# A twelve-slot loop under a hand-written lane schedule: three slots of rest after the reciprocal root, statistics and normalising in pairs of tiles, one scaling step on GpSimd, and another background pace

## The chip, the cores and the metric

The kernel runs on one core of one Trainium2 chip. The metric is the device time of one execution in microseconds (us); the time before is 6226.83 us, the median of 5 runs (6213.99 to 6240.11).

## The reference, cut to what matters

Eight images of 128 channels and 36 by 36 positions pass through a convolutional attention layer (layer 0), and then, as 1296 tokens of 128 channels, through an additive attention and a gated mixture of experts (layer 1).

```
x = x + conv_attention(group_norm(x))            # 3x3 convolutions, softmax attention, tanh
t = to_tokens(x)
t = t + additive_attention(layer_norm(t))        # softmax over j of sum_d w_d tanh(q_id + k_jd)
t = t + experts(layer_norm(t))                   # 64 experts, each takes its 8 likeliest tokens
x = from_tokens(t)
```

The experts' gating takes a softmax over the 1296 tokens for each expert, keeps the 8 largest probabilities and uses them as weights.

## The kernel before, in words

**The main loop.** The additive attention is written as sums of fractions: a denominator and a numerator, both matrix products of exponentials of queries and keys. It is cut into 8 images (`b`), 3 chunks of 432 queries (`c`) and 11 key tiles (`j`). Such a unit has 12 *slots*, the short eleventh tile (16 keys, placed sixth in the order) has 3, so an image has 3 x (10 x 12 + 3) = 369 slots and the kernel 2952. Slots are numbered here from 0 to 368 within an image; slots 60 to 62, 183 to 185 and 306 to 308 are the short ones. In each slot `p` the program emits:

1. `take_turns(p)`: steps of the background work that need no matmul (VectorE, ScalarE, GpSimd),
2. `numerators(p)`: PE products into two PSUM tiles `n`, from a ring `ps_n` of 4 that the background's PSUM tiles (`aux`) share,
3. `denominators(p + 3)`: PE products into a tile `d`, then on ScalarE a logarithm `lq` (line 872) and, in every second slot, exp(-lq) for both (line 875),
4. `terms(p)`: VectorE multiplies `n` by `lq`. In the slots 0, 1, 3, 4, 6, 7, 9, 10 of a unit the two results `rp` (line 903, ring of 3) are added by GpSimd (lines 908, 910); in the slots 2, 5, 8, 11 (`DVE_PAIRS`) VectorE adds them itself (lines 892 to 899),
5. `matmul_turn(p)`: steps of the background work that start with matmuls.

Each engine runs its instructions in the order in which they were emitted, so a step that waits holds up all that stands behind it on that engine.

**The background work.** While image `b` goes through the main loop, lanes of Python generators emit the rest of the work a step at a time: the gating of image `b - 1` (lane `gates`), and for image `b + 1` in turn `normal`, `conv_keys`, `layer0`, `tokens` and `keys` (lane `background`). A generator says with each `yield` what it wants next: `step(r)` is a step without matmuls after `r` slots of rest, `matmuls(r)` a step that begins with matmuls after `r` slots, `TAKE` is `step(1)`. Every background matmul adds its columns plus 20 to a counter; `matmul_turn` lets one group through when the balance is not negative, and gives the balance `PACE` columns back in each slot:

```
            before = behind[0]
            for lane in lanes:
                while lane.due(p, True) and behind[0] == before:
                    if lane is not first_of_all and balance[0] < 0 or lane is gates and urgent:
                        break
                    lane.run(p)
            balance[0] = min(balance[0] - (behind[0] - before) + PACE, PACE)
```

`layer0(b + 1)` emits nothing until the gating of `b - 1` is through. Image 0 is prepared ahead of the loop; the last image's gating, and the experts, come behind it.

**The parts that the change touches.** `tokens` turns an image into tokens: 11 transposes (`tpl`) in groups of 4 tiles, copies into `tok` (line 558), then for each of the 11 tiles a `bn_stats` and a `bn_aggr` on VectorE (lines 573, 574), with a `step()` behind every third tile; then `ve` (variance plus epsilon, line 216), two slots of rest, the reciprocal root `ln_rs` on GpSimd (line 221), transposes `tpn` and the normalising `xh` on VectorE (line 593), four tiles at a time, then the transposes `tpc` and copies `xT` (line 610). `gate_logits` does the like with the attention's result: `tp3`, and the normalising at line 739, four tiles at a time, once for each of the three chunks. `gate_tokens` has the softmax over tokens: the maximum `nm` (line 766), an exp on ScalarE with its sum (line 769), a reciprocal `ginv` (line 772), the scaling of the 64 x 1296 probabilities `probs` on ScalarE (line 774), the 8 largest (`Max8`, line 777) and their replacement (line 780) on VectorE, and a difference on GpSimd (line 782). The tanh of `layer0` (line 464, between two loads of ScalarE's function tables) is not touched; neither is `normal`, whose `xwin` (lines 353 to 357) are GpSimd additions.

Of the kernel before, what the change touches and what calls it, by code (L numbers as in the profile page):

```python
# [10 lines left out]
AF = mybir.ActivationFunctionType  # L11
ALU = mybir.AluOpType
AX = mybir.AxisListType

NB, C, H, W = 8, 128, 36, 36
# [7 lines left out]
T = 108  # L23
NT = N // T
TPC = CH // T
KT = [(j, min(128, N - j)) for j in range(0, N, 128)]
NKT = len(KT)
# [28 lines left out]
LAG = 3  # L56
SHIFT = 6.5
DVE_PAIRS = (2, 5, 8, 11)
PACE = 350

REM_SLOTS = [([q + m for m in range(NF // 2)], rows) for q, rows in SLOTS[:3]]

# [2 lines left out]
def kernel(  # L65
# [28 lines left out]
    nc = tc.nc  # L94
# [21 lines left out]
    ident = const.tile([128, 128], F32, tag="ident", name="ident")  # L116
# [4 lines left out]
    with ExitStack() as loop, ExitStack() as score:  # L121
# [22 lines left out]
        def big_tile(name):  # L144
            return big.tile([128, NT * 128], F32, tag="big", name=name)
# [4 lines left out]
        def aux(name):  # L150
            return ps_n.tile([128, 512], F32, tag="n", name=name)
# [76 lines left out]
        TAKE = (False, 1)  # L228

        def step(rest=1):  # L230
            return (False, rest)

        def matmuls(rest=0):
            return (True, rest)
# [7 lines left out]
        def turned_to(out, in_, identity):  # L242
            behind[0] += 148
            nc.tensor.transpose(out, in_, identity)
# [294 lines left out]
        def tokens(b):  # L539


            r = xs.pop(b)
            tok = big_tile("tok")[:, : NKT * C].rearrange("p (t c) -> p t c", c=C)
            st = small.tile([128, NKT, 6], F32, tag="ln_st", name="ln_st")
            mv = small.tile([128, NKT, 2], F32, tag="ln_mv", name="ln_mv")
            nc.gpsimd.memset(mv, 1.0)
            yield matmuls(2)
            for g in range(0, NKT, 4):
                tp = aux("tpl")
                some = list(range(g, min(g + 4, NKT)))  # L550
                for t in some:
                    o, n = KT[t]
                    turned_to(
                        tp[:n, (t - g) * C : (t - g + 1) * C], r[:, o : o + n], ident
                    )
                yield TAKE
                full = sum(KT[t][1] == 128 for t in some)
                nc.vector.tensor_copy(
                    tok[:, g : g + full, :],
                    tp[:, : full * C].rearrange("p (t c) -> p t c", c=C),  # L560
                )
                for t in some[full:]:
                    n = KT[t][1]
                    nc.vector.tensor_copy(tok[:n, t, :], tp[:n, (t - g) * C : (t - g + 1) * C])
                yield matmuls()
            full = N // 128
            nc.sync.dma_start(
                tokd[b][: full * 128].rearrange("(t p) c -> p t c", p=128), tok[:, :full, :]
            )
            o, n = KT[-1]  # L570
            nc.sync.dma_start(tokd[b][o : o + n], tok[:n, NKT - 1, :])
            for t, (o, n) in enumerate(KT):
                nc.vector.bn_stats(st[:n, t, :], tok[:n, t, :])
                nc.vector.bn_aggr(mv[:n, t, :], st[:n, t, :])
                if t % 3 == 2:
                    yield step()
            ve = plus_eps(mv[:, :, 1], 1e-5, [128, NKT])
            yield step(2)
            rs = small.tile([128, NKT], F32, tag="ln_rs", name="ln_rs")
            rsqrt(rs, ve)  # L580
            xh = big_tile("xh")[:, : NKT * (C + 1)].rearrange("p (t c) -> p t c", c=C + 1)
            nc.gpsimd.memset(xh[:, :, C : C + 1], 1.0)
            yield matmuls()
            for g in range(0, NKT, 4):
                tp = aux("tpn")
                some = list(range(g, min(g + 4, NKT)))
                for t in some:
                    o, n = KT[t]
                    turned_to(tp[:n, (t - g) * C : (t - g + 1) * C], r[:, o : o + n], ident)
                yield TAKE  # L590
                for t in some:
                    n = KT[t][1]
                    nc.vector.tensor_scalar(  # L593
                        xh[:n, t, :C], tp[:n, (t - g) * C : (t - g + 1) * C],
                        mv[:n, t, 0:1], rs[:n, t : t + 1], ALU.subtract, ALU.mult,
                    )
                yield matmuls()
            xT = big_tile("xT")[:, :N]
            yield matmuls(2)
            for g in range(0, NKT, 4):  # L600
                tp = aux("tpc")
                some = list(range(g, min(g + 4, NKT)))
                for t in some:
                    o, n = KT[t]
                    turned_to(
                        tp[:, (t - g) * 128 : (t - g) * 128 + n], xh[:n, t, :C], ident[:n, :n]
                    )
                yield TAKE
                lo, hi = KT[g][0], KT[some[-1]][0] + KT[some[-1]][1]
                nc.vector.tensor_copy(xT[:, lo:hi], tp[:, : hi - lo])  # L610
                yield matmuls()
            xr = two.tile([128, C + 1], F32, tag="xr", name="xr")
            for i in range(TPC):
                nc.sync.dma_start(xr[32 * i : 32 * i + REM], xh[:REM, NKT - 1, :])
            prepared[b] = (xh, xT, xr)
# [39 lines left out]
        def attend(b, c, es):  # L655
# [38 lines left out]
            if b == NB - 1:  # L694
                yield from gate_logits(b, [c])
# [7 lines left out]
        def gate_logits(b, chunks):  # L703


            t2, mv = attended[b]
            if b not in logits:
                logits[b] = (
                    big_tile("probs")[:E, :N],
                    small.tile([E, NCH], F32, tag="mx", name="mx"),  # L710
                )
            pr, mx = logits[b]
            tiles = range(chunks[0] * TPC, (chunks[-1] + 1) * TPC)
            yield step()
            ve = plus_eps(mv[:, tiles[0] : tiles[-1] + 1, 1], 1e-5, [T, len(tiles)])
            yield step(2)
            rs = small.tile([T, len(tiles)], F32, tag="t2_rs", name="t2_rs")
            rsqrt(rs, ve)
            yield matmuls()

            def turned(c, name):
                tp = aux("tp2")
                for j in range(TPC):
                    turned_to(tp[:, j * T : (j + 1) * T], t2[:T, c * TPC + j, :], ident[:T, :T])
                return tp, chunk_tile(name)

            for c in chunks:
                tp, tt = turned(c, "t2T")
                yield TAKE
                nc.vector.tensor_copy(tt, tp[:, :CH])  # L730
                nc.sync.dma_start(t2d[b][:, c * CH : (c + 1) * CH], tt)
                yield matmuls(1)
                tp = aux("tp3")
                for j in range(TPC):
                    turned_to(tp[:T, j * C : (j + 1) * C], tt[:, j * T : (j + 1) * T], ident)
                yield TAKE
                for j in range(TPC):
                    t = c * TPC + j
                    nc.vector.tensor_scalar(
                        t2[:T, t, :], tp[:T, j * C : (j + 1) * C],  # L740
                        mv[:, t, 0:1], rs[:, t - tiles[0] : t - tiles[0] + 1],
                        ALU.subtract, ALU.mult,
                    )
                yield matmuls(1)
            for c in chunks:
                tp, xc = turned(c, "xc")
                yield TAKE
                nc.vector.tensor_copy(xc, tp[:, :CH])
                yield matmuls(2)
                pg = aux("pg")  # L750
                bmm(pg[:E, :CH], gw_s, xc, start=True, stop=True)
                yield TAKE
                nc.vector.tensor_scalar(
                    pr[:, c * CH : (c + 1) * CH], pg[:E, :CH], gb_s, None, ALU.add, ALU.max,
                    accum_out=mx[:, c : c + 1],
                )
                yield matmuls()

        def gate_tokens(b):


            t2, _ = attended.pop(b)
            pr, mx = logits.pop(b)
# [7 lines left out]
            inv = small.tile([E, 1], F32, tag="ginv", name="ginv")  # L771
            nc.vector.reciprocal(inv, tot)
            yield step()
            nc.scalar.activation(pr, pr, AF.Copy, scale=inv)
            yield step(2)
            top = small.tile([E, 8], F32, tag="top", name="top")
            nc.vector.max(out=top, in_=pr)
            yield step()
# [8 lines left out]
            for g in range(2):  # L787
                tp = aux("tpg")
                for j in range(half):
                    t = g * half + j  # L790
# [172 lines left out]
        def matmul_turn(p):  # L963
# [3 lines left out]
# [7 lines that stand above are left out]
# [17 lines left out]
        for p, (u, k) in enumerate(slots):  # L991
            b, c, j = units[u]
# [216 lines left out]
```

## Time and profile before

| what | value |
|---|---|
| time, median of 5 runs | 6226.83 us |
| the profiled execution's own time | 6213.99 us |
| its span | 6212.3 us |
| mean granted TensorE clock | 0.974 |
| PE busy | 5972.8 us (96%) |
| ScalarE (ACT) busy | 5348.4 us (86%) |
| VectorE (DVE) busy | 4831.3 us (78%) |
| GpSimd (POOL) busy | 4698.0 us (76%) |

The profiled execution was the fastest of the five. Engine times are of instructions that overlap in a pipeline, so a busy PE need not be working at its peak. The granted clock is the share of TensorE's full clock that the chip let it have; it is either 1 or one half at any moment of this profile. A main-loop unit with no background work at all is found in the last image, where nothing is left to prepare.

### The profile page before, as it was taken

Reading aid. Unit: us, or ns where it says so; the run is one execution under the profiler, and the core shown is the slowest. Engines: PE = TensorE matmul, PEld = TensorE weight load, DVE = VectorE, ACT = ScalarE, POOL = GpSimd, SP = SyncE. Lnnn points to the kernel's source line nnn. Section 1 sums busy time; section 2 is a strip of 40 time slices with the busy share of each in tenths; the row PEclk is TensorE's granted clock in tenths of the full one; section 3 lists DMA queues with packets and bytes.
Section 4 is the critical chain, followed back from the end, with each engine's and each line's share of the span. In section 5 each row is a group of like instructions: output and inputs, shape, how many; then the busy total and the mean of one; then the engine's idle time right before and its main releaser. Section 6 shows DMA issues by size and latency. Waiting matters only on the chain.

```text
span 6212.3 us, 108419 instructions
## 1 busy us (share of the span) xinstructions
PE 5972.8 (96%) x41064; PEld 2930.5 (47%) x41064; DVE 4831.3 (78%) x9595; ACT 5348.4 (86%) x5426; POOL 4698.0 (76%) x2868
## 2 busy tenths in 40 slices
PE   7899999999999999999999999999999999999996
PEld 5454455544554445544445444554445444544443
DVE  3687778877788777887788787887778878788872
ACT  1799998998989989899898998899888998999980
POOL 3678877787788877888687786778777887778870
PEclk9999999999999999999999999999999999999997
DMA  1210021100110001100111001110011000100018
GB/s 43 70 36 22 23 66 38 34 25 28 58 52 23 26 30 65 37 27 23 50 45 42 22 21 62 41 36 22 24 65 48 24 26 27 59 31 29 25 58 272
DMA packets 158892, 272.37 MB, mean 44 GB/s; under 512 B 53857, under 2 KB 83425, under 8 KB 158369
## 3 DMA queue, kind: packets, MB, share of 16 engines
q1 hardware_dynamic: 158368, 265.44, 13.0%
q8 instruction: 323, 5.29, 0.4%
q14 instruction: 201, 1.64, 0.1%
HBM read 200.94 MB, written 64.19 MB: 43 GB/s over the span
## 4 chain that ended last, share of the span: by engine, by line
PE 75%; DVE 9%; ACT 6%; issue 6%; POOL 2%; DMA 1%; SPq 0%; DVEq 0%; POOLq 0%; ACTq 0%
PE n L850 36%; PE d L850 11%; PE pa L240 7%; PE pc L240 5%; ACT lq L872 4%; DVE n L897 3%; PE s L240 3%; PE pk L240 3%; PE pq L240 2%; DVE rp L903 2%; DVE accd L899 1%; PE n L857 1%; PE d L857 1%; POOL accp L910 1%; DMA w<-in_weight_dram 1%
## 5 line engine op out<-in xcount | busy, mean ns | idle before, releaser
L910 POOL TENSOR_TENSOR accp<-accp,rp 128x864 f32<-128x864 f32 x1464 | 2966.2, 2026 | 1006.7 <-DVE rp L903 942.2
L850 PE MATMUL n<-qf,kf 32*128 32x432 f32 (+1 forms) x11520 | 3279.0, 575 | 63.0 <-DVE xh L593 14.5
L872 ACT ACTIVATE lq<-d 128x864 f32<-128x864 f32 x2952 | 2552.9, 882 | 504.5 <-PE d L850 461.6
L850 PE MATMUL d<-qf,kf 32*128 32x432 f32 (+1 forms) x11520 | 2874.3, 565 | 39.4 <-ACT lq L872 34.8
L903 DVE TENSOR_TENSOR rp<-n,lq 128x432 f32<-128x432 f32 x3984 | 2198.5, 600 | 562.1 <-PE d L850 392.9
L875 ACT ACTIVATE lq<-lq 128x1728 f32<-128x1728 f32 x1488 | 2430.0, 1633 | 47.1
L850 PEld LDWEIGHTS n<-qf,kf 32*128 32x128 f32 (+1 forms) x11520 | 1186.0, 185 | 1605.0 <-DVE rp L903 451.0
L850 PEld LDWEIGHTS d<-qf,kf 32*128 32x128 f32 (+1 forms) x11520 | 1031.5, 187 | 406.1 <-issue 230.9
L897 DVE TENSOR_TENSOR n<-n,lq 128x432 f32<-128x432 f32 x1440 | 811.9, 609 | 263.9 <-PE n L850 228.9
L899 DVE TENSOR_TENSOR accd<-n,accd 128x432 f32<-128x432 f32 x1440 | 868.0, 603 | 24.7
L908 POOL TENSOR_TENSOR accp<-rp 128x864 f32<-128x864 f32 x264 | 534.4, 2024 | 145.5 <-DVE rp L903 143.7
L917 POOL TENSOR_TENSOR accp<-accp 128x432 f32<-128x432 f32 x264 | 291.7, 1105 | 17.6
L648 POOL TENSOR_SCALAR qf<-qf,cs_s 128x432 f32<-128x432 f32 x192 | 261.3, 1367 | 43.2 <-ACT qf L647 43.2
L240 PEld LDWEIGHTS pa<-xh,e 128*108 128x108 f32 x1920 | 223.6, 175 | 131.2 <-DVE rp L903 76.6
L920 POOL TENSOR_TENSOR accd<-accp,accd 128x432 f32<-128x432 f32 x240 | 266.0, 1108 | 21.9 <-DVE accd L899 3.8
L240 PE MATMUL pa<-xh,e 128*108 128x129 f32 x1920 | 262.8, 284 | 10.3 <-DVE accd L899 6.1
L892 DVE TENSOR_TENSOR accd<-n,lq 128x432 f32<-128x432 f32 x240 | 144.8, 603 | 113.3 <-PE n L850 83.5
L240 PE MATMUL s<-q,k 128*116 128x432 f32 x480 | 230.3, 568 | 2.2 <-DVE q L272 1.4
L426 ACT ACTIVATE e<-s 116x432 f32<-116x432 f32 x240 | 125.0, 521 | 119.0 <-PE s L240 118.7
L240 PEld LDWEIGHTS pk<-xT,a_k 128*128 128x128 f32 x1408 | 171.7, 193 | 106.7 <-issue 27.5
L417 POOL TENSOR_TENSOR tot<-tot,e 116x432 f32<-116x432 f32 x192 | 212.3, 1106 | 6.7 <-ACT e L426 4.5
L240 PE MATMUL pa<-e,vw 116*128 116x432 f32 x480 | 204.6, 549 | 2.8 <-DVE accd L899 2.8
(202 smaller groups left out, 3963.8 us busy)
## 6 DMA issues: line engine op xcount, KB each, us to landing
kf<-kd SPq DMA_DIRECT2D x240, 512.0 KB
kd<-ks SPq DMA_DIRECT2D x160, 256.0 KB
w<-in_weight_dram SPq DMA_DIRECT2D x32, 1024.0 KB
wk_t<-wk_t_d SPq DMA_DIRECT2D x7, 768.0 KB
wv_t<-wv_t_d SPq DMA_DIRECT2D x7, 768.0 KB
wq_t<-wq_t_d SPq DMA_DIRECT2D x7, 768.0 KB
x<-in_x_dram SPq DMA_DIRECT2D x8, 648.0 KB
t<-tokd SPq DMA_DIRECT2D x96, 54.0 KB
```

What stands on the lines that cost most here:

```text
L240: mm(out, lhsT, rhs, **kw)
L648: nc.gpsimd.tensor_scalar(qf[:, 1, :], qf[:, 0, :], cs_s[:, q : q + 1], None, ALU.mult)
L850: mm(outs[h][:, :CH], kf[rows[h], q, :], qf_of[b, c, q][rows[h], part, :], start=True, stop=True)
L872: nc.scalar.activation(lq[:, o : o + 2, :], d[:, :, :CH], AF.Ln)
L875: nc.scalar.activation(some, some, AF.Exp, scale=-1.0)
L897: mult(ns[h], ns[h], lq[:, o + h, :])
L899: nc.vector.tensor_add(live["d"], ns[h], live["d"])
L903: mult(rp[:, h, :], ns[h], lq[:, o + h, :])
L908: nc.gpsimd.tensor_add(live["p"], live["r"], rp)
L910: nc.gpsimd.tensor_add(live["p"], live["p"], rp)
L917: nc.gpsimd.tensor_add(s[:, 0, :], s[:, 0, :], s[:, 1, :])
L920: nc.gpsimd.tensor_add(d, s[:, 0, :], d)
```

## The change

In `tokens`, the statistics pass on after every second tile; three slots lie between the reciprocal root and the first normalising transposes (none before), and transposing and normalising go two tiles at a time. In `gate_logits`, the normalising goes two tiles at a time. In `gate_tokens`, the scaling of the probabilities is a GpSimd instruction for all images but the last, and three slots lie behind it in place of two. `PACE` goes from 350 to 365 columns a slot.

```diff
-PACE = 350
+PACE = 365
...
                 nc.vector.bn_stats(st[:n, t, :], tok[:n, t, :])
                 nc.vector.bn_aggr(mv[:n, t, :], st[:n, t, :])
-                if t % 3 == 2:
+                if t % 2 == 1:
                     yield step()
...
             nc.gpsimd.memset(xh[:, :, C : C + 1], 1.0)
-            yield matmuls()
-            for g in range(0, NKT, 4):
+            yield matmuls(3)
+            for g in range(0, NKT, 2):
                 tp = aux("tpn")
-                some = list(range(g, min(g + 4, NKT)))
+                some = list(range(g, min(g + 2, NKT)))
...
-                tp = aux("tp3")
-                for j in range(TPC):
-                    turned_to(tp[:T, j * C : (j + 1) * C], tt[:, j * T : (j + 1) * T], ident)
-                yield TAKE
-                for j in range(TPC):
-                    t = c * TPC + j
-                    nc.vector.tensor_scalar(
-                        t2[:T, t, :], tp[:T, j * C : (j + 1) * C],
-                        mv[:, t, 0:1], rs[:, t - tiles[0] : t - tiles[0] + 1],
-                        ALU.subtract, ALU.mult,
-                    )
-                yield matmuls(1)
+                for j0 in range(0, TPC, 2):
+                    tp = aux("tp3")
+                    for j in (j0, j0 + 1):
+                        turned_to(tp[:T, j * C : (j + 1) * C], tt[:, j * T : (j + 1) * T], ident)
+                    yield TAKE
+                    for j in (j0, j0 + 1):
+                        t = c * TPC + j
+                        nc.vector.tensor_scalar(
+                            t2[:T, t, :], tp[:T, j * C : (j + 1) * C],
+                            mv[:, t, 0:1], rs[:, t - tiles[0] : t - tiles[0] + 1],
+                            ALU.subtract, ALU.mult,
+                        )
+                    yield matmuls()
...
-            nc.scalar.activation(pr, pr, AF.Copy, scale=inv)
-            yield step(2)
+            if b == NB - 1:
+                nc.scalar.activation(pr, pr, AF.Copy, scale=inv)
+            else:
+                nc.gpsimd.tensor_scalar(pr, pr, inv, None, ALU.mult)
+            yield step(3)
             top = small.tile([E, 8], F32, tag="top", name="top")
             nc.vector.max(out=top, in_=pr)
```

## The prediction

> **What bounds the kernel now.** I read the page first, then cut the loop into its units (the starts of line 872, one a slot, give the borders) and asked for busy times and granted clock in each. The windows view gives, in order: a unit without background (last image), and in image 3 the units of slots 294 to 305 (tanh), 309 to 320 (statistics, normalising), 48 to 59 (gating's softmax) and the short unit behind it.
>
> ```profile
> core 0: us, PE busy (x) PEld busy (x) DVE busy (x) ACT busy (x) POOL busy (x), PEclk, DMA share, GB/s
> 5740.08:5760.04 19.96, 19.25 (x98) 7.68 (x98) 16.73 (x32) 19.77 (x20) 16.61 (x10) 1.00 0.08 27
> 2984.92:3015.02 30.10, 26.51 (x352) 12.04 (x348) 21.53 (x40) 25.67 (x24) 18.00 (x13) 0.89 0.09 33
> 3020.91:3051.41 30.50, 26.36 (x115) 12.13 (x110) 24.81 (x66) 21.18 (x21) 19.45 (x13) 0.78 0.16 48
> 2499.36:2524.29 24.93, 24.87 (x363) 12.86 (x360) 22.48 (x44) 23.52 (x23) 23.18 (x20) 1.00 0.09 29
> 2524.29:2534.34 10.05, 9.53 (x152) 5.56 (x150) 4.61 (x10) 4.13 (x4) 5.34 (x4) 0.66 0.05 12
> ```
>
> A bare unit is ScalarE's: 19.77 of 19.96 us. With background a unit lasts 21 to 25 us, bound by whichever engine has most in it; PE's 96% hides that. Two units stick out at 30 us, and the clock falls there: 0.78 over 30.50 us is 2 x 0.22 x 30.5 = 13.4 us at half clock. The unit of the change is the third row. Its chain is in the timeline (image 2's copy of it, VectorE then GpSimd) and the waits:
>
> ```profile
> 2288.37 1.13 DVE L897 TENSOR_TENSOR n<-n,lq 128x432 f32<-128x432 f32 x2 [0.59 <-PE n L850]
> 2289.40 1.24 DVE L899 TENSOR_TENSOR accd<-n,accd 128x432 f32<-128x432 f32 x2
> 2293.15 1.37 DVE L593 TENSOR_SCALAR xh<-tpn,ln_mv,ln_rs 128x128 f32<-128x128 f32 x4 [2.50 <-POOL ln_rs L221]
> ```
>
> ```profile
> 2286.89 4.12 POOL L910 TENSOR_TENSOR accp<-accp,rp 128x864 f32<-128x864 f32 x2 [2.94 <-DVE rp L903]
> 2290.97 2.15 POOL L221 TENSOR_TENSOR ln_rs<-ve,neg_half 128x11 f32<-128x11 f32 x1
> ```
>
> ```profile
> DVE xh L593 <- POOL ln_rs L221: 20.0, 8, 2.7
> ```
>
> The root stands behind two additions on GpSimd, VectorE stands 2.5 us before `xh` with the main loop's products behind it, and PE then stands 2.4 us (the largest gaps before it are 1.16 and 0.71 us, behind the statistics). All 8 images wait so.
>
> **Part 1, tokens.** Work is unchanged: 11 x (0.266 + 0.182) = 4.9 us of statistics and 11 x 0.40 = 4.4 us of `xh`. Before, VectorE has 24.81 us to do in the 30.50: 5.7 us over, of which 2.5 is the wait and 3.2 the half clock and the gaps.
> - Rest: the root has three slots (about 6 us against 2.15 plus two additions of 2.03). The wait of 2.5 goes. Next late is VectorE itself: 9.3 main + 4 us for the six slots of `xh`, which is about what it does now.
> - Pairs of `xh`: 0.8 us a slot in place of 1.6. With the wait gone I let the second half-clock stretch go, half of 3.2 less gaps: -1.6. Six `aux` tiles instead of three tighten the ring `ps_n`; bounds -0.3 to +1.5, taken 0, since VectorE is the limit there.
> - Statistics: the built order shows six tiles in a row become four (not two: one turn is run by `matmul_turn`, the next by the following `take_turns`), then twos. 2.4 us of burst become 1.6, 1.2 become 0.8: -1.2 of gaps.
> - Against it: the statistics now stand in slots 300 to 304, with no background up to slot 309. VectorE has 13.6 us for six slots (9.0 main, 4.6 statistics) where PE alone would take 10: a half-clock stretch is likely to stay and now reaches the short unit 306 to 308. What a stretch costs there: the short unit 60 to 62 lasts 7.0 us in image 2 (clock 1), 10.05 in image 3. Bounds 0 to +3, taken +1.3.
> Sum: -2.5 - 1.6 - 1.2 + 1.3 = -4.0 us an image, bounds -7 to -1. The tanh unit (third of a stretch of the same kind) only moves, nine slots ahead.
>
> One rule on the clock differs from these rows. The Trainium skill (TensorE: Matmul & The Clock Gate, "HAM oscillation — how this bites in real kernels") asks for PE gaps over about 3.4 us before the clock falls. Here it falls after gaps of 1.16 and 0.71 us, so gaps alone don't decide. By the page no clock would be won, and part 1 would be -2.5 - 1.2 = -3.7.
>
> **Part 2, gating's normalising.** Slots 24 to 35 last 24.9 us in image 2 (clock 1) and 26.6 in image 3 (6.8 us at half clock). Four `L739` of 0.402 in a row, among three `bn_stats` of 0.6, become twos. The stretch was full in three images of six; -0.7, bounds -1.7 to +0.5. The transposes use the same slots (28 to 37), so gating is not later: `tpg` at slot 65, before 66.
>
> **Part 3, the scaling.** ScalarE loses 1.36 us in a unit where it is busy 23.52 of 24.93: -1.0. GpSimd gains a one-input pass over 1296 columns, which the trace lacks. Nearest rows:
>
> ```profile
> L648 POOL TENSOR_SCALAR qf<-qf,cs_s 128x432 f32<-128x432 f32 x192 | 261.3, 1367 | 43.2 <-ACT qf L647 43.2
> L782 POOL TENSOR_TENSOR gt<-probs,gt 64x1296 f32<-64x1296 f32 x7 | 20.6, 2937 | 0.0
> ```
>
> Three times the first is 4.1 us, the second 2.9. I take 3.6 (1.367 x 2.937/1.105, the width's ratio taken from lines 782 and 917). GpSimd is behind there, in GpSimd's, ScalarE's and VectorE's timelines:
>
> ```profile
> 2512.67 4.13 POOL L910 TENSOR_TENSOR accp<-accp,rp 128x864 f32<-128x864 f32 x2
> ```
>
> ```profile
> 2517.43 1.36 ACT L774 ACTIVATE probs<-probs,ginv 64x1296 f32<-64x1296 f32 x1
> ```
>
> ```profile
> 2519.56 1.49 DVE L777 MAX8 top<-probs 64x8 f32<-64x1296 f32 x1
> ```
>
> The scaling is emitted behind the additions that end at 2516.8; the last `xwin` group comes a slot later than before, so I place their end at 2517.5 and the scaling's at 2521.1. `Max8` stays in slot 59 and could start at 2519.4: VectorE stands 1.7 us (0.3 to 3), with slot 59's products behind it, and PE's `n` behind those. The half clock in the short unit, full in two of six images and half in two, becomes the rule: +1.2. Sum +1.9, bounds -1 to +5. In the last image no `xwin` is in the way: 0.
>
> A page prices it otherwise. The Trainium skill (GPSIMD Engine Reference, "4.1 Engine selection") holds one-input passes to be roughly line rate there, which would be an estimate of 1.5 us from the `Max8` row; then nothing waits, the part is -1.0, and the whole would be near 6189.
>
> **Part 4, pace.** Columns don't change (117752 an image), their places do. In the built order `keys` ends at slot 357, not 363. Units with the same load in the trace give the exchange: slots 270 to 281 fall from 4520 to 3164 columns (25.3 to 22.3 us, -3.0), slots 345 on give another -1.5; units at 75, 87, 123, 147, 186 and 246 take 390 to 820 more, worth +0.2 to +1.5 each, +4.8 together, and the smaller moves -0.9. Sum -0.6, bounds -3 to +3.
>
> **Sum.** -4.0 - 0.7 + 1.9 - 0.6 = -3.4 us in each of images 1 to 6, -20 us in all. Image 0 has no gating (part 1 gain and pace loss cancel), image 7 has no tokens: 0 each. The profiled time 6214.0 becomes 6194; it lies 12.8 below the median of 6226.8, so on that scale 6206.
>
> **Rivals.**
> - *GpSimd becomes the wait (slower).* Place: slot 59. It decides once the scaling ends 3 us or more after VectorE arrives. Then part 3 is +5, the half clock stays behind the statistics (part 1 -1.5) and pace gives +0.5: 6 x 4 = +24, 6251; milder forms end near 6242. For it: GpSimd 23.18 of 24.93 us busy before the addition. Against: the rest is three slots. Chance 0.25.
> - *All half clock goes.* Statistics in twos keep PE fed, `Max8` doesn't wait: part 1 -7, part 2 -1, part 3 -0.5, pace 0: -8 x 6 = -48, 6179 to 6190. For it: short gaps triggered these stretches. Against: 13.6 us of VectorE in six slots. Chance 0.22.
> - *The change doesn't thin the bursts enough.* Four tiles in a row and an idle background keep the stretch: part 1 -2, the rest as forecast: -1.4 x 6 = -8, 6218. Chance 0.19.
>
> **How the numbers follow.** The forecast of 6206 has 0.34. About 0.2% (12.5 us) is what a measurement of this kernel can tell from no change: below 6214 is faster, over 6239 slower. Faster 0.34 + 0.22 = 0.56; same 0.19; slower 0.25. The range reaches from the second rival's low end to the milder forms of the first: 6178 to 6246.
>
> **What would show it.** Right: no wait of `xh` for `ln_rs`; the unit of slots 309 to 320 at 24 to 25 us with a clock of 1; the mean clock up from 0.974 to about 0.98; the scaling at 3.5 to 4.1 us with a wait of `Max8` for it near 1.7. Wrong: a wait of `Max8` over 3 us, the clock at half in slots 300 to 308 in every image for 6.8 us, or units at 75 to 250 longer by more than 5 us in sum.

## The result and the profile after

| | before | after |
|---|---|---|
| time, median (runs) | 6226.83 us (57) | 6238.84 us (32) |
| profiled execution, span | 6212.3 us | 6250.2 us |
| mean granted clock | 0.974 | 0.972 |

The ratio is 1.0018, 95% interval 1.0011 to 1.0024: some 11 us slower, where 6206 had been forecast. The profiled execution of before lies 12.8 us below its median, that of after 13.2 us above; 26 of the 38 us between the two traces are scatter.

The windows view of after, in the order of the rows shown of before (bare unit; image 3: 294 to 305, 309 to 320, 48 to 59, the short unit 60 to 62), with the unit of slots 24 to 35 as a last row:

```profile
core 0: us, PE busy (x) PEld busy (x) DVE busy (x) ACT busy (x) POOL busy (x), PEclk, DMA share, GB/s
5801.54:5821.50 19.96, 19.25 (x98) 7.68 (x98) 16.73 (x32) 19.77 (x20) 16.34 (x10) 1.00 0.08 27
3004.73:3029.59 24.86, 23.27 (x351) 11.63 (x347) 24.26 (x60) 21.32 (x21) 16.08 (x11) 0.93 0.21 68
3036.18:3058.86 22.68, 22.42 (x122) 10.88 (x119) 21.42 (x45) 20.67 (x21) 18.45 (x12) 1.00 0.11 32
2509.79:2536.25 26.46, 26.29 (x364) 13.87 (x360) 22.51 (x44) 22.44 (x22) 26.18 (x23) 1.00 0.09 31
2536.25:2543.21 6.96, 6.43 (x152) 3.68 (x150) 4.64 (x10) 4.13 (x4) 5.31 (x4) 1.00 0.02 5
2460.44:2488.17 27.73, 25.16 (x120) 11.70 (x120) 26.23 (x54) 20.95 (x20) 20.65 (x13) 0.94 0.13 43
```

The unit of the change, 309 to 320, went from 30.50 to 22.68 us, with the clock at 1. Unit 24 (slots 24 to 35) did not get shorter; before, it was in this image:

```profile
2450.80:2477.44 26.64, 24.96 (x124) 11.80 (x121) 24.62 (x54) 20.80 (x20) 19.66 (x12) 0.87 0.25 92
```

VectorE's waits, and the scaling in the groups and in GpSimd's and VectorE's timelines:

```profile
DVE xh L593 <- POOL ln_rs L221: 2.3, 1, 2.3
DVE top L781 <- POOL probs L778: 1.2, 6, 0.2
```

```profile
L778 POOL TENSOR_SCALAR probs<-probs,ginv 64x1296 f32<-64x1296 f32 x7 | 24.9, 3554 | 0.0
```

```profile
2527.92 3.55 POOL L778 TENSOR_SCALAR probs<-probs,ginv 64x1296 f32<-64x1296 f32 x1
```

```profile
2531.51 1.50 DVE L781 MAX8 top<-probs 64x8 f32<-64x1296 f32 x1 [0.19 <-POOL probs L778]
```

The 20 us wait of `xh` is down to one of 2.3 (image 0), and `Max8` waits 0.2 us a time. To see where the time went I summed the unit lengths by stretch of an image (borders are again the starts of the logarithm's line), the mean of images 1 to 6, in brackets the time at half clock:

| kernel | 0-23 | 24-62, gating | 63-281 | 282-320, tokens | 321-368 | image |
|---|---|---|---|---|---|---|
| before | 45.5 | 81.2 (8.0) | 428.9 (0.6) | 88.4 (18.8) | 97.8 | 741.8 |
| after | 45.1 | 84.4 (9.1) | 434.2 (2.3) | 83.9 (18.2) | 99.3 | 746.9 |

The tokens stretch gained 4.5 us an image; gating lost 3.2, and slots 63 to 281 and 321 to 368, which hold none of the edited steps, lost 6.8.

How much of this is scatter can be told from the kernel before_psum (below), whose time is that of before while its profiled execution lies 18 us above its median: nearly all of its units without half clock last as long as in before within 0.15 us, but its tokens stretch takes 90.9 us, with 25.0 at half clock. So 2 or 3 us in the gating and tokens stretches can be scatter of the clock; the 6.8 us are not.

In unit 24 the trace of after shows something new. VectorE's timeline in image 3, then GpSimd's and PE's:

```profile
2475.43 0.15 DVE L318 COPY gm<-pm 128x1 f32<-128x1 f32 x1
2475.61 0.54 DVE L320 TENSOR_TENSOR dev<-gn_mv,gm 128x1 f32<-128x1 f32 x1
2476.19 2.05 DVE L321 SCALAR_TENSOR_TENSOR dev<-dev,gn_mv 128x1 f32<-128x1 f32 x1
2478.16 1.12 DVE L901 TENSOR_TENSOR n<-n,lq 128x432 f32<-128x432 f32 x2
```

```profile
2474.12 4.11 POOL L914 TENSOR_TENSOR accp<-accp,rp 128x864 f32<-128x864 f32 x2 [1.98 <-DVE rp L907]
```

```profile
2479.84 0.62 PE L854 MATMUL n<-qf,kf 32*128 32x432 f32 x1 [1.79 <-DVE accd L903]
```

Lines 318 to 321 belong to `normal`, the group statistics of the next image: mean `gm` from PSUM tile `pm`, deviation `dev`, its square plus variance. Each handles one value a lane. In the same image of before they took 0.15 to 0.22 us, in a pause of GpSimd (VectorE's timeline, then GpSimd's):

```profile
2470.76 0.22 DVE L321 SCALAR_TENSOR_TENSOR dev<-dev,gn_mv 128x1 f32<-128x1 f32 x1
```

```profile
2465.50 4.10 POOL L910 TENSOR_TENSOR accp<-accp,rp 128x864 f32<-128x864 f32 x2 [1.94 <-DVE gn_mv L312]
2472.83 2.02 POOL L910 TENSOR_TENSOR accp<-accp,rp 128x864 f32<-128x864 f32 x1 [3.23 <-DVE rp L903]
```

In after, line 320 ends at 2476.15, when GpSimd's first addition ends (2474.12 plus one of 2.03), and line 321 at 2478.24, when the second ends (2478.23). The main loop's products stand behind, PE is idle for 1.79 us, and half clock follows. It is so while images 1 to 6 pass through the main loop of after (2.05 us), and in image 0 alone of before (1.88 us). In the built order of image 3 the matmul `pm` stands in slot 31 and no longer in slot 32, so the small work went from slot 33, where GpSimd pauses, into slot 32.

### The profile page after: what moved, and what is told of

Its sections match the earlier page's. It is cut to its first block, busy times and chain, and to the rows that moved or that the text cites. A ratio compares the mean times of both kernels' runs of the same rounds, so it can differ in the third digit from the quotient of the medians.

```text
span 6250.2 us, 108342 instructions
## 1 busy us (share of the span) xinstructions
PE 6002.3 (96%) x41064; PEld 2946.3 (47%) x41064; DVE 4843.9 (78%) x9595; ACT 5342.7 (85%) x5419; POOL 4722.3 (76%) x2875
## 4 chain that ended last, share of the span: by engine, by line
PE 65%; DVE 12%; ACT 9%; issue 7%; POOL 5%; DMA 1%; SPq 0%; POOLq 0%; DVEq 0%; ACTq 0%
PE n L854 30%; PE d L854 10%; PE pa L240 6%; ACT lq L876 6%; PE pc L240 5%; DVE n L901 4%; DVE rp L907 4%; PE s L240 3%; PE pk L240 3%; DVE accd L903 2%; POOL accp L914 2%; PE pq L240 2%; ACT lq L879 1%; PE n L861 1%; PE d L861 1%
## 5 line engine op out<-in xcount | busy, mean ns | idle before, releaser
L854 PE MATMUL d<-qf,kf 32*128 32x432 f32 (+1 forms) x11520 | 2905.6, 565 | 42.5 <-ACT lq L876 35.3
L854 PEld LDWEIGHTS d<-qf,kf 32*128 32x128 f32 (+1 forms) x11520 | 1049.8, 187 | 410.8 <-issue 223.0
L924 POOL TENSOR_TENSOR accd<-accp,accd 128x432 f32<-128x432 f32 x240 | 266.1, 1109 | 24.9 <-DVE accd L903 3.9
```

The lines of the kernel that those rows point to most:

```text
L854: mm(outs[h][:, :CH], kf[rows[h], q, :], qf_of[b, c, q][rows[h], part, :], start=True, stop=True)
L924: nc.gpsimd.tensor_add(d, s[:, 0, :], d)
```

## The experiments

The first theory (A) put the loss on the allowance, `PACE`, its rival (B) on the gating's edits; later letters name the theories that followed. Ratios are against before on the same chip, with 95% intervals.

| kernel | median us | ratio |
|---|---|---|
| pace | 6259.52 | 1.0065 (1.0048 to 1.0082) |
| tokens_354 | 6204.27 | 0.9965 (0.9953 to 0.9977) |
| tokens_365 | 6233.63 | 1.0010 (0.9997 to 1.0023) |
| scaling | 6217.15 | 0.9988 (0.9978 to 0.9997) |
| after_354 | 6213.70 | 0.9974 (0.9963 to 0.9986) |
| after_shifted | 6236.09 | 1.0010 (1.0001 to 1.0019) |
| after_psum_operands | 6212.02 | 0.9977 (0.9965 to 0.9989) |
| tokens_scaling_354 | 6211.24 | 0.9968 (0.9957 to 0.9980) |
| pace_psum | 6244.63 | 1.0036 (1.0020 to 1.0052) |
| before_psum | 6224.90 | 1.0003 (0.9990 to 1.0017) |
| after_354_psum | 6204.52 | 0.9972 (0.9958 to 0.9985) |
| pairs | 6278.36 | 1.0086 (1.0070 to 1.0102) |
| tanh_later | 6257.98 | 1.0049 (1.0036 to 1.0061) |
| after_without_pairs | 6249.64 | 1.0027 (1.0014 to 1.0040) |
| after_without_scaling | 6242.33 | 1.0022 (1.0010 to 1.0033) |
| tokens_scaling_354_psum | 6206.93 | 0.9970 (0.9960 to 0.9979) |
| pace_psum_tanh_back | 6217.71 | 0.9981 (0.9969 to 0.9994) |
| tokens_354_psum | 6201.37 | 0.9961 (0.9948 to 0.9975) |

### One part alone

**pace**: only the allowance.

```diff
-PACE = 350
+PACE = 365
```

> The kernel before with the allowance raised from 350 to 365 and nothing else. Theory A (the allowance is what eats the gain: it packs the background work of an image more tightly, and the units outside the gating and tokens stretches got some 5 us per image longer between the two traces): with the rests and pairs absent nothing is given back, so 6226.8 + 6 x 5 = 6257 us, between 6245 and 6270, and units 87 to 246 each 0.5 to 2 us longer than before with no half clock in them. Theory B (the allowance is about neutral, as the prediction's part 4 had it at -0.6 us per image, and the loss comes from the gating's edits): 6223 us, between 6215 and 6232. In both the tokens stretch keeps its wait for xh and a half-clock stretch, 10 or so slots earlier in the image.

Measured 6259.52 us. The size is theory A's, the place is not: slots 63 to 281 took 430.7 us (+1.8) and 321 to 368 took 95.1 (-2.7). What grew is gating (83.3), the tokens stretch (93.1, 22.2 at half clock) and image 0 (735.0 to 750.1; one execution each).

**tokens_354**: the tokens hunks of the change alone, with `PACE = 354`.

> The kernel before with the tokens part alone (statistics in pairs, rest of three, xh pairs) at an allowance of 354, about the smallest at which the keys of the next image are still there in time. Theory A: 6226.8 - 6 x 5 for the tokens stretch + 6 x 1.5 for the four of fifteen allowance units = 6206 us, between 6198 and 6216. Theory B: 6226.8 - 6 x 4 = 6203 us, between 6195 and 6212. The two do not part here; a time at or above 6222 would speak against both, and against part 1 of the prediction.

Measured 6204.27 us, faster by 0.35%, as both theories had it. The windows view of slots 309 to 320 in image 3:

```profile
3034.18:3055.18 21.00, 20.78 (x111) 9.39 (x104) 19.76 (x43) 20.03 (x20) 17.95 (x13) 1.00 0.02 5
```

**tokens_365**: the same with `PACE = 365`.

> The tokens part alone at the change's allowance of 365; gating as before. Theory A: the tokens stretch gives 30 us and the allowance takes 30 us, 6227 us, between 6218 and 6236. Theory B: 6203 us, between 6195 and 6212, as at 354. The distance between this kernel and the one at 354 is what eleven units of allowance cost: 20 us by A, nothing by B.

Measured 6233.63 us: theory A. Eleven units of allowance cost 29 us; by the traces an image loses 3.8 us in gating and 3.8 in the tokens stretch, and gains 4.2 in slots 63 to 281. The operation of line 321 took 0.22 us in images 1 to 6 of tokens_354 and 2.05 us in all six here: the allowance had moved it.

**scaling**: only the hunk of `gate_tokens`, `PACE = 350`.

> The kernel before with the probabilities' scaling on GpSimd (all images but the last) and a rest of three behind it, allowance 350. Prediction's part 3: +1.9 us x 7 = 6240 us, with Max8 waiting 1 to 3 us. Theory A (the page after shows Max8 waiting only 0.2 us a time, so it costs little): 6226.8 + 0 to 6, say 6229 us. Theory B (the loss is in the gating's edits, this one among them): 6226.8 + 7 x 2.5 = 6244 us, between 6236 and 6252.

Measured 6217.15 us, faster than any theory had it. The short unit 60 to 62 lasts 6.6 us in the mean (8.5 before), with 0.6 us at half clock (3.4).

**pairs**: only the hunk of `gate_logits`, `PACE = 350`.

> The kernel before with the gating's normalising in pairs and nothing else, allowance 350. Prediction's part 2: 6227 - 7 x 0.7 = 6222 us, bounds 6215 to 6230. Theory A: the pairs cost little, 6221 to 6233 us, the small operation staying at 0.22 us. Theory B: they cost 2 us per image, 6241 us, between 6236 and 6250.

Measured 6278.36 us, and none had that. The windows view, slots 24 to 35 and 294 to 305 of image 3:

```profile
2481.89:2506.41 24.52, 23.28 (x122) 11.05 (x118) 24.28 (x53) 20.61 (x20) 19.72 (x12) 1.00 0.28 102
3017.38:3051.42 34.04, 31.07 (x347) 13.76 (x345) 20.49 (x38) 25.25 (x24) 17.90 (x12) 0.75 0.05 16
```

The unit of the pairs got shorter (25.2 us in the mean, 25.9 before). Most of the time is lost elsewhere: 270 slots later in tanh's unit (32.2 against 29.7 us in the mean), and in slots 63 to 281 (432.8 against 428.9, with 5.1 us at half clock against 0.6). In the built order the pairs end gating's matmuls later, and as the background of the next image shares the balance, `po0`, the products behind tanh, goes from slots 300-302 to 302-304.

### The meeting on VectorE

**after_shifted**: one slot of rest ahead of the small work; the other positions in images 1 to 6 stay.

```diff
             yield TAKE
+            yield step()
             gm = small.tile([C, 1], F32, tag="gm", name="gm")
```

> The change with one slot of rest ahead of the group statistics' small VectorE work, so that it lies in slot 33 as before and not in 32; the rest of the order stays. Theory C (there its 128x1 operation with two operands in the shared memory stands behind GpSimd's 4.12 us additions, 2.05 us and not 0.22, so VectorE's accumulation waits, TensorE idles and half clock follows): unit 24 falls from 28 to 25 us in images 1 to 6, 6239 - 6 x 3 = 6221 us, between 6214 and 6228. Rival D (the 1.8 us is hidden; the unit's length comes from the halved transposes): the operation shrinks to 0.22 us and the time stays, 6236 to 6242 us.

**after_psum_operands**: same slot, other operands.

```diff
-            nc.vector.tensor_sub(dev, mv[:, 0:1], gm)
-            nc.vector.scalar_tensor_tensor(dev, dev, dev, mv[:, 1:2], ALU.mult, ALU.add)
+            nc.vector.tensor_sub(pm[:, 1:2], mv[:, 0:1], pm[:, :1])
+            nc.vector.scalar_tensor_tensor(dev, pm[:, 1:2], pm[:, 1:2], mv[:, 1:2], ALU.mult, ALU.add)
```

> The change with the same small work in the same slot 32, but with the mean taken from the accumulation memory pm and the deviation written there (pm's column 1), so that the operation that took 2.05 us has one operand in the shared memory and not two. If the length comes from two such operands meeting GpSimd's addition: 0.2 to 0.4 us and the time of the shifted kernel, about 6221 us. If it comes from the slot itself (a wait that the record counts as the operation's length): 2.05 us still, 6236 to 6242 us.

The second one first: 6212.02 us, 0.41% below after in the ratios (1.0018 to 0.9977), about 25 us. VectorE's and GpSimd's timelines in image 3:

```profile
2468.86 0.15 DVE L320 TENSOR_TENSOR pm<-gn_mv,pm 128x1 f32<-128x1 f32 x1
2469.05 0.22 DVE L321 SCALAR_TENSOR_TENSOR dev<-pm,gn_mv 128x1 f32<-128x1 f32 x1
```

```profile
2467.48 4.12 POOL L914 TENSOR_TENSOR accp<-accp,rp 128x864 f32<-128x864 f32 x2 [2.00 <-DVE rp L907]
```

GpSimd's pair of additions covers the operations as before, and they take 0.15 and 0.22 us. So it is the two operands in SBUF (the expectations' shared memory; PSUM is their accumulation memory), not the slot. This agrees with the Trainium skill (SBUF — State Buffer, "🔬 SBUF: two separate sides"): a VectorE instruction with two SBUF inputs needs a port pair that a GpSimd instruction reading SBUF holds for its whole length, and whoever comes second blocks fully. In the trace of after, line 320 began 1.5 us into the first addition and ended with it. Unit 24 took 23.9 us in the mean (28.2 in after).

In after_shifted the operation is short too:

```profile
2490.59 0.22 DVE L322 SCALAR_TENSOR_TENSOR dev<-dev,gn_mv 128x1 f32<-128x1 f32 x1
```

Gating in images 1 to 6 fell to 80.6 us (-3.8), as theory C had it, yet the time was 6236.09 us and not 6221. In its trace image 0, whose background has come a slot later too, is 11.2 us longer, with 23 us more at half clock; there the operation now meets GpSimd (1.88 us, 0.22 in after). That takes back half of the 23 us. The rest the traces cannot place: they lie 21.5 us apart where the medians lie 3, since after's execution was 13 us above its median and this one 6 below. So this run by itself doesn't bear out theory C's price.

**before_psum**: the control, the same operands in before.

> The kernel before with these operands alone. There the operation took 1.88 us only in image 0 and 0.22 us in the others, so theory E expects 6227 us less 0 to 4, between 6221 and 6229. If the operands are worth something by themselves, without the meeting (rival F), it is about 27 us faster as in the change: 6200 us.

6224.90 us, no difference: where the meeting is in image 0 alone, the operands are worth nothing that can be measured.

**pace_psum**: they with the allowance alone.

> The kernel before with the allowance at 365 and the small group statistics' operands in the accumulation memory; nothing else. Theory E (most of the allowance's +33 us is the meeting in slot 32, priced at 27 us between the change and its version with these operands): 6259.5 - 27 = 6232 us, between 6226 and 6240. Rival F (the allowance costs by packing more into the tokens stretch and image 0, and the meeting is small here): 6250 to 6260 us.

6244.63 us, between E and F: of the allowance's 34 us (40 by the ratio) the meeting is 15 to 18. Gating is at 79.5 us an image, but the tokens stretch at 95.5.

### The place of tanh

**tanh_later**: nothing but two slots of rest.

```diff
-            yield step(2)
+            yield step(4)
             nc.scalar.activation(hp, hp, AF.Tanh, bias=hb)
```

> The kernel before with two slots more of rest ahead of tanh, nothing else: tanh, the tokens stretch and what follows in images 1 to 6 lie exactly where the pairs alone put them (po0 in slots 302 to 304, tpl 307 to 310), and the gating is that of before. Theory G (the pairs' price is the place of tanh and the tokens stretch among the units; unit 294's half clock went from 6.8 to 17.1 us there): 6226.8 + 6 x 4 = 6251 us, between 6243 and 6262, unit 294 at 34 us. Rival H (the pairs themselves cost, in the middle stretch or by contention): 6222 to 6234 us, unit 294 at 30 us.

6257.98 us: theory G, 27 to 31 us for two slots of tanh and of the tokens stretch behind it. PE's wait behind tanh in image 3, before and then tanh_later, and windows of 7 us from the fall of the clock on, in the same order:

```profile
2997.59 1.81 PE L850 MATMUL d<-qf,kf 32*128 32x432 f32 x4 [2.97 <-ACT lq L872]
```

```profile
3012.41 0.99 PE L850 MATMUL d<-qf,kf 64*128 64x432 f32 x4 [2.97 <-ACT lq L872]
```

```profile
2996.00:3003.00 7.00, 5.41 (x15) 1.70 (x16) 1.81 (x4) 6.92 (x7) 2.02 (x1) 0.55 0.00 0
3003.00:3010.00 7.00, 7.00 (x112) 3.26 (x117) 5.75 (x11) 4.32 (x4) 2.84 (x2) 0.96 0.01 2
```

```profile
3013.00:3020.00 7.00, 7.00 (x76) 3.16 (x72) 3.96 (x7) 5.49 (x6) 1.65 (x1) 0.54 0.01 2
3020.00:3027.00 7.00, 7.00 (x76) 2.81 (x74) 2.46 (x4) 2.71 (x3) 3.28 (x4) 0.50 0.00 0
```

In both, tanh with its two table loads holds ScalarE for 4 us, PE stands 2.97 us for a logarithm, and the clock halves. Before, it is back after 6.8 us; two slots later it stays at half for 13.7 us (3013.5 to 3027.2) although PE is busy in all of them. What PE does there is in its timeline:

```profile
3019.11 1.81 PE L240 MATMUL po<-hpre,w_o 128*128 128x432 f32 x2
3020.85 1.81 PE L850 MATMUL n<-qf,kf 32*128 32x432 f32 x4
3022.59 1.69 PE L857 MATMUL d<-qf,kf 32*32 32x108 f32 x64
```

Line 857 has the denominators of the short unit, 64 products on 32 by 32 corners of the array, emitted three slots ahead, in slots 303 to 305. Before, the half clock ends 4 us ahead of them; later, it runs into them. That such small products let the clock stay down is a reading, not shown.

**pace_psum_tanh_back**: pace_psum with `step(15)` there, which gives `po0`, `tpl`, `tpn` and `tpc` in images 1 to 6 the slots of before.

> The kernel before at an allowance of 365 with the group statistics' operands in the accumulation memory, and thirteen slots more of rest ahead of tanh, which puts po0, tpl, tpn and tpc in the very slots of before (300 to 323). Theory G (what is left of the allowance's price is the place of tanh's stretch, 95.5 against 88.4 us in slots 282 to 320, and image 0's): 6245 - 18 = 6227 us, between 6219 and 6235. Rival I (the allowance costs by packing, wherever tanh stands): 6240 to 6250 us.

6217.71 us, below theory G's value: the place of tanh and the tokens stretch together was 25 us by the distances from before, 34 by the ratios, and nothing is left that the allowance would cost by packing. Slots 294 to 305 in image 3, pace_psum and then this kernel:

```profile
3012.38:3047.77 35.39, 29.70 (x353) 15.00 (x350) 27.30 (x70) 21.35 (x20) 20.38 (x14) 0.76 0.13 40
```

```profile
2995.85:3025.54 29.69, 26.54 (x345) 11.57 (x344) 19.78 (x37) 25.44 (x24) 18.16 (x13) 0.89 0.07 20
```

### What the parts are worth inside the change, and the fastest version

**after_354** (the change with `PACE = 354`) and **after_354_psum** (with the operands in PSUM too):

> The whole change with the allowance at 354 and not 365. Theory A, mended by the first runs (at 365 the small group statistics of image b+1 move from slot 33 into slot 32, where they meet GpSimd's additions, and the gating and tokens stretches each lose 3 to 4 us per image against the tokens part at 354; the gating's edits cost little): 6204 us, as the tokens part alone at 354, between 6195 and 6215. Theory B (the gating's edits cost 2 us per image whatever the allowance): 6204 + 12 = 6216 us, between 6211 and 6225.

> The whole change at 354 with these operands. At 354 the operation stands in slot 34 and took 1.88 us in images 3 to 7. Theory E: 6213.7 - 5 x 1.5 to 4 = 6200 us, between 6192 and 6207, the fastest so far beside the tokens part at 354. Rival F: 6210 to 6216 us.

6213.70 and 6204.52 us. The first lies between A's value and B's, nearer B's; its operation stands in slot 34 and took 1.88 us in images 0 and 2 to 6 of the main loop (the statistics of images 1 and 3 to 7). The second is at E's value by its median, but the ratios (0.9974 and 0.9972) do not part the two: at this place the meeting has no price that shows, though by their intervals one of some 10 us could hide.

**after_without_pairs** and **after_without_scaling**:

> The change at 365 with the gating's normalising in one go of four, as before. The order puts tanh's stretch 3 slots earlier without the pairs (po0 in 287 and not 290). Theory G: the pairs' price is a matter of place, so no fixed sign; the tokens part at 365 took 6234 us at this place, and GpSimd's scaling took 9 off before: 6225 to 6234 us. Rival H (pairs cost 53 us wherever they are): 6239 - 53 = 6186 us.

> The change at 365 with the probabilities' scaling back on ScalarE; the order of everything else stays. Prediction's part 3 (scaling on GpSimd costs 1.9 us an image): 6239 - 13 = 6226 us. By the run of the scaling alone (8.8 us faster than before): 6239 + 9 = 6248 us, between 6240 and 6256.

6249.64 and 6242.33 us. Taking the pairs out does not make the change faster (0.1% slower, with intervals that overlap), so the pairs' 53 us do not hold at any place, as G has it; the time is 16 us above G's range, though. The scaling is worth nothing that can be measured here (1.0022 without, 1.0018 with).

**tokens_scaling_354**, the same with PSUM operands, and **tokens_354_psum**:

> The tokens part and GpSimd's scaling at 354, without the gating's normalising in pairs. From the two kernels by themselves (tokens part -21.7 us, scaling -8.8 us, each against before): 6226 - 30 = 6196 us if they add, 6204 us if the scaling's gain was the half clock of unit 60 that the tokens part at 354 removes anyway. Against the whole change at 354 it tells what the pairs cost: by theory B some 6 to 12 us, by A under 4.

> The tokens part and GpSimd's scaling at 354 with the group statistics' operands in the accumulation memory, without pairs: the version that the runs point to. At 354 without pairs the operation met nothing in images 1 to 7 (0.22 us), so the operands bring only image 0's 1.7 us: 6211 - 2 = 6209 us, between 6200 and 6213. If the operands are worth 27 us here too: 6184 us.

> The tokens part alone at 354 with the group statistics' operands in the accumulation memory. Without the meeting in images 1 to 7 the operands bring only image 0's 1.7 us: 6203 us, between 6196 and 6209. If they are worth more by themselves: under 6190 us.

6211.24, 6206.93 and 6201.37 us: the scaling adds nothing to the tokens part, and the operands nothing where the meeting is absent. The tokens part at 354, with or without PSUM operands, has the lowest ratios of the study, 0.35 to 0.39% below before and about 0.55% below after.

## Why the prediction was wrong

**Part 1 held.** -4.0 us an image forecast, -4.5 in after's tokens stretch, and the tokens part alone at 354 is 22 us faster, 3.6 an image. The wait is gone, unit 309 has its full clock, and a stretch at half clock did stay in slots 294 to 308 (11.4 us in the mean). "The tanh unit only moves" left out a price: here its unit lasts 28.0 us at slot 282 where it was 29.7 at 294, but tanh_later and pace_psum_tanh_back show that its place can cost 25 us and more over the run.

**Part 2: the unit right, the sentence on its place wrong.** Without the meeting the pairs' unit is 0.7 us shorter alone and 2.0 in after_psum_operands; -0.7 was forecast. But "gating is not later" looked at the transposes of gating only. By themselves the pairs put tanh two slots later; tanh_later shows that two slots cost 27 to 31 of the 53 us. The 3.9 us an image in slots 63 to 281 I can't assign.

**Part 3: the price of the scaling right, its three terms not.** The scaling took 3.55 us (3.6 taken; the estimate from the page, 1.5, did not hold). The wait of `Max8`, 1.7 us an image, was 0.2. The short unit did not fall to half clock as a rule (+1.2; in after it lasts 8.2 us in the mean, 8.5 before). ScalarE's relief (-1.0) does not show either: with the scaling alone slots 48 to 59 take 24.9 us, as before. In after they take 26.5, but 26.2 with the scaling back on ScalarE and 24.8 without the pairs: slots 36 to 47 take 21.5 us with the pairs and 23.0 without, so the pairs shift 1.5 us by a unit. The part has no loss, and alone it gained 8.8 us. GpSimd's additions did not push it: it ended 0.2 us behind VectorE's arrival. The first rival, the slower one, fell with it: slower came true by another mechanism.

**Part 4 is the step that failed.** It priced the allowance as an exchange of columns, -0.6 us an image; alone, the allowance costs 34 us (40 by the ratio). With the allowance alone the exchange itself was right: slots 63 to 281 and 321 to 368 sum to 526.7 us before and 525.8 then, -0.9. But columns were taken for the whole price of a move. The allowance also put two things into other neighbours' way: line 321's small operation beside GpSimd's additions (15 to 18 us alone, 25 in the change) and tanh's gap, with the tokens stretch behind it, into another place (25 to 34 us alone; not measured in the change). Neither is in the sum or the rivals.

In the change the exchange did not hold either: the same slots sum to 533.5 us, +6.8. The six units that were to get longer did so by 5.0 us (+4.8 forecast), but slots 270 to 281 gave back 1.4 (3.0 forecast) and those from 345 on 0.6 (1.5), and slots 171 to 182 and 321 to 344, which were not in the sum, lost 2.1 each. Two of the prediction's signs of being wrong came true with it: the units from 75 to 257 are 6.2 us longer in sum, and slots 300 to 308 have 6.8 us or more at half clock in each of images 1 to 6.

With the meeting taken away the change runs in 6212 us, 6 from the forecast, and that is in part luck: in its trace these slots still lose 5.7 us an image, which the tokens stretch (-5.2 against -4.0) and gating (-1.4 against +1.2) make up.

**What stays open.** In after and in tokens_354 slots 63 to 281 and 321 to 368 are 6 to 7 us an image longer than before, with little half clock; that work moved there out of the tokens stretch is likely but not shown. Why the shifted kernel gained so little, and why PE stays at half clock while busy, is open too.

## What to carry to other kernels

When a schedule's pace changes, list what each moved instruction meets in its new slot, also the ones that take 0.2 us: here a VectorE operation with two SBUF operands beside a GpSimd addition ended with that addition (2.05 us and not 0.22), and taking one operand from PSUM removed that. A part's gain is known only at its place: the same pairs cost 53 us alone and nothing that shows within the change. Price a pace by building it at the smallest value that still works, since here 354 kept the gain that 365 lost.

## What the runs showed of the hardware that was not expected

- A 128x1 VectorE operation with two SBUF operands took 2.05 us beside a GpSimd addition, 0.22 us with its operand in PSUM at the same overlap.
- The clock stayed at half for 27.3 us in tokens_365 with PE busy throughout (windows view):

```profile
3017.50:3044.80 27.30, 27.30 (x430) 13.82 (x430) 16.74 (x34) 14.06 (x14) 15.00 (x10) 0.51 0.09 26
```

  The Trainium skill (TensorE: Matmul & The Clock Gate, "What's actually happening") has the full clock back after one busy window of some 3.4 us; by these records, where busy is modelled, it wasn't.

- Over the twenty traces, an image's length (mean of images 1 to 6) follows its time at half clock with 0.47 us for each us and a correlation of 0.88. That many of the schedule's moves act through the clock is a reading of this; a correlation doesn't show which comes first, and the 6.8 us above came with little half clock.
